# A recurrence over a graph: first gates' inputs copied earlier, one round fewer in the last sub-block, base sums spread 2,1,2,2,2,2,2,3, and another order of the filler tasks

## The chip, the core and the metric

The kernel runs on one core of a Trainium2 chip. The metric is the device time of one execution in microseconds, the median of several runs. A profile is one execution; its span is the time from the first to the last instruction.

## What is computed

Four layers work on node features `x` [16, 1024, 256] and a weighted adjacency `adj` [16, 1024, 1024]; each layer adds its result to `x`, after a layer norm and a ReLU. The change touches layer 2 only, a recurrence over the nodes in their order:

```python
norm_adjT = jnp.swapaxes(adj, 1, 2) * dinv[:, :, None]

def step(h, i):
    x = jnp.take(h_e, i, axis=1)
    row = jnp.take(norm_adjT, i, axis=1)
    x_par = jnp.einsum('bj,bjd->bd', row, h)
    iou = x @ W_ioux.T + b_ioux + x_par @ W_iouh.T + b_iouh
    r, z = jnp.split(iou, 2, axis=1)
    r, z = (jax.nn.sigmoid(r), jax.nn.sigmoid(z))
    hc = jnp.tanh(x @ W_coux.T + b_coux + x_par * r @ W_couh.T + b_couh)
    h_new = z * x_par + (1.0 - z) * hc
    h = jax.lax.dynamic_update_slice(h, h_new[:, None, :], (0, i, 0))
    return (h, None)
h_out, _ = jax.lax.scan(step, h_e, jnp.arange(n))
```

About 3% of the entries of `adj` are not zero, so most nodes that stand near each other don't depend on each other.

## The kernel before

Layers 0 and 1 run from the start to about 1510 us, the recurrence to about 3455 us, layer 3 to the end. Everything is float32.

**Blocks and sub-blocks.** The 1024 nodes are 8 blocks (`t`) of 128. Within a block the nodes of each batch element are put into an order, worked out on the chip from `adj` (`orders`), and cut into 8 sub-blocks (`s`) of 16 nodes; for 16 batch elements a sub-block has 256 columns. Nodes that depend on each other are kept in different sub-blocks where that is possible. Where it isn't, a sub-block holds chains of nodes, and a chain of n nodes needs n rounds: a round (`round_`, from line 831) computes gates and new states of all columns from the present guess of `x_par`.

**Rounds.** `KS` (line 27) says how many rounds of each sub-block stand in the program, `CUTS` (line 28) at which column the second and later rounds begin, since the first nodes of a chain are done by then. For the eighth sub-block these are five rounds: one of 16 columns per batch element, two from column 4 on, two from column 12 on. If a block's data need more, `one_more` (line 876) repeats a whole round of all 256 columns, under the `If` of lines 1014 to 1017. How many are needed is in `more`, computed by `orders` from the chains.

**Order of work.** The order on PE, DVE, ACT and POOL is the order in which the Python code issues instructions (`tc.manual_schedule`, line 898). In each round PE has matmuls for `pr` and `pz` (each 4, recorded as 8 in a profile), then ACT and DVE make the sigmoid and the product for `pc`'s right side, PE does `pc`, ACT the tanh, DVE `w` and `hT` (lines 860, 861), PE four transposes (`turned`, line 865), ACT copies to `h` or `dh`. While ACT and DVE do their part PE is given other work from a list of tasks, `todo`. `fill(weight)` (line 953) takes tasks from it in order: a share before the first round, a share behind `pc`, the rest behind the transposes. The kinds of tasks, by the names used below:

- *base* (line 637): one of the matmuls that sum the earlier and later blocks' states for the next block, a chain of seven for one batch element, and a *turn* (line 651), two transposes. `BASES` (line 29) says how many batch elements each sub-block has. Base reads `hb`, which is loaded by SP's DMA queue, in part from `hs_d`, where the last sub-block's states of the block before have just been scattered (line 1030, POOL).
- *gates* (line 749): `x @ W` for a later sub-block, three tasks, each read from `hs`, a copy that POOL makes (line 740) of one sub-block of `he`.
- *far* (line 784): what the sub-block just done gives to later columns of the same block; *last* (line 687): what the last sub-block of the block before gives.
- *next* (line 771): what a sub-block gives to the first sub-block of the next block, into `pnx`.

Each base chain, turn, gates, far and last task holds one of three PSUM tiles named `pf`, from its first matmul until DVE or ACT has evicted it. The evictions (line 787 on DVE for far, 652 for turn, 624 on ACT for base) are put into a list, `late`, and issued at `evict()`, which stands before the sigmoids, behind the last `hT`, and behind the copies to `h`.

The gates of sub-blocks 2 to 7 and of the next block's first are issued at the end of the sub-block before, in the two arms of the `If`. Those of sub-block 1 are made in the gaps of sub-block 0: `Gates(he, 1)` at line 936 issues POOL's two copies there, and the three tasks come behind the first six base tasks. POOL's queue also carries the scatters, the gathers of `aj` (line 714), masks of `ab` (line 615) and the products `bd`, `ai` (lines 730, 721).

Of the kernel before, what the change touches and what calls it, by code (L numbers as in the profile page):

```python
# [16 lines left out]
P = 128  # L17
# [4 lines left out]
S = 16  # L22
NS = P // S
G2 = 2
GB = B // G2
GR = GB * S
KS = (1, 1, 1, 1, 1, 2, 2, 5)
CUTS = {5: (8,), 6: (8,), 7: (4, 4, 12, 12)}
BASES = (1, 1, 2, 2, 2, 2, 2, 4)
LN_EPS = 1e-5  # L30
RMS_EPS = 1e-6
DEG_EPS = 1e-5
# [8 lines left out]
def gnn_stack(ctx: ExitStack, tc: tile.TileContext, a: dict, out: bass.AP):  # L41
# [65 lines left out]
    def orders(pool, psum):  # L107
# [9 lines left out]
        def tile_(name, n=P):  # L117
            return pool.tile([P, n], F32, name="o_" + name)
# [39 lines left out]
        def rest():  # L158
# [47 lines left out]
            found = tile_("held", S)[:, :1]  # L206
            for s, cuts in CUTS.items():
                for k, cut in enumerate(cuts):
# [21 lines left out]
            for s in range(NS):  # L230
                nc.vector.scalar_tensor_tensor(need[:, s], again[:, s], float(KS[s] - 1), need[:, s], op0=ALU.mult, op1=ALU.add)
            for k in range(2):
                left = pool.tile([1, NT, NS], F32, name="o_left")
                for s in range(NS):
                    nc.vector.tensor_scalar(left[:, :, s], need[:, s], float(KS[s] + k), 0.0, op0=ALU.subtract, op1=ALU.max)
                nc.vector.tensor_copy(more[k], left.rearrange("o t s -> o (t s)"))
# [325 lines left out]
    def layer_2(shared, early):  # L562
        with ExitStack() as st:
# [102 lines left out]
            def last_tasks(t, bxt):  # L666

                n = P - S
                loaded = {}

                def load(b0):
                    ao = big.tile([P, 4, n], F32, name="ao", bufs=3)
                    nc.sync.dma_start(ao, next_d[b0 : b0 + 4, t - 1].rearrange("b p i -> p b i"))
                    hr = big.tile([P, 4, D], F32, name="hr", bufs=3)
                    nc.sync.dma_start(hr, hs_d[t - 1][b0 // GB][b0 % GB * P : (b0 % GB + 4) * P]
                                      .rearrange("(b p) d -> p b d", p=P))
                    loaded[b0] = ao, hr

                def task(b):
                    def run():  # L680
                        b0 = b - b % 4
                        ao, hr = loaded[b0]
                        if b % 4 == 0 and b + 12 < B:
                            load(b + 12)
                        pl = psum.tile([P, DC, n], F32, name="pf", bufs=3)
                        for c in range(DC):
                            nc.tensor.matmul(pl[:, c], hr[:, b - b0, c * P : (c + 1) * P], ao[:, b - b0],
                                             start=True, stop=True)
                        to = bxt[:, :, b, S:]
                        return lambda: nc.vector.tensor_add(to, to, pl)  # L690
                    return 0.4, run
                for b0 in (0, 4, 8):
                    load(b0)
                return [task(b) for b in range(B)]

            def load_he(t):
                he = big.tile([P, DC, B, P], F32, name="he")
                for c in range(DC):
                    nc.sync.dma_start(he[:, c], heT_d[:, :, c, t * P : (t + 1) * P].rearrange("b p i -> p b i"))
                return he  # L700
# [66 lines left out]
            def next_block(h, bd, n, start):  # L767

                for c in range(DC):
                    for g in range(G2):  # L770
                        nc.tensor.matmul(pnx[:, c, g * GR : (g + 1) * GR], h[:, g, c * P : (c + 1) * P],
                                         bd[:, g, :, n : n + S], start=start and c == 0 and g == 0, stop=True,
                                         skip_group_check=True)

            def far_tasks(bxt, h, sub):


                bd, s = sub.bd, sub.s
                far = P - (s + 2) * S

                def task(g, c, b4):
                    def run():
                        pf = psum.tile([P, 4, far], F32, name="pf", bufs=3)
                        nc.tensor.matmul(pf, h[:, g, c * P : (c + 1) * P], bd[:, g, b4 : b4 + 4, S : S + far],  # L784
                                         start=True, stop=True)
                        to = bxt[:, c, g * GB + b4 : g * GB + b4 + 4, P - far :]
                        return lambda: nc.vector.tensor_add(to, to, pf)  # L787
                    return 0.0067 * far, run
                tasks = []
                if far > 0:  # L790
                    tasks = [task(g, c, b4) for g in range(G2) for c in range(DC) for b4 in (0, 4)]
                if sub.n > P - s * S:
                    tasks.append((0.9, lambda: next_block(h, bd, P - (s + 1) * S, s == 0)))
                return tasks


# [68 lines left out]
            def turned(hT, fill, to):  # L865

                ph = psum.tile([P, DC, G2, P], F32, name="pa")
                for e in range(DC):
                    for g in range(G2):
                        nc.tensor.transpose(ph[:, e, g], hT[:, e, g * GR : (g + 1) * GR], ident)  # L870
                fill()
                for e in range(DC):
                    nc.scalar.activation(to[:, :, e * P : (e + 1) * P], ph[:, e], AF.Copy)
                evict()
# [23 lines left out]
            with tc.manual_schedule(engines={mybir.EngineType.PE, mybir.EngineType.DVE, mybir.EngineType.Activation, mybir.EngineType.Pool}):  # L898
                he = load_he(0)
# [12 lines left out]
                gx.seed_r()  # L912
                gx.seed_zc()

                near = None
                behind = []
                for t in range(NT):
                    if t == NT - 1:
# [9 lines left out]
                    for s in range(NS):  # L928


                        ahead = (t, s + 1) if s + 1 < NS else (t + 1, 0)
                        K = KS[s]
                        share = [task for _ in range(BASES[s] if base_todo else 0) for task in base_todo.popleft()]
                        todo, gx_next = [], None
                        if s == 0:
                            gx_next = Gates(he, 1)
                            todo = share[:6] + [(1.72, task) for task in gx_next.tasks] + share[6:] + behind
                        else:
                            if s == 1 and t + 1 < NT:
                                he_next = load_he(t + 1)  # L940
                            if s == 1 and t > 0:
                                for g in range(G2):
                                    nc.sync.dma_start(hn_d[g * GB : (g + 1) * GB, (t - 1) * P : t * P],
                                                      hs_d[t - 1][g].rearrange("(b p) d -> b p d", p=P))
                            lists = [behind, share]
                            sizes = [len(x) for x in lists]
                            while any(lists):
                                i = max(range(2), key=lambda i: len(lists[i]) / max(sizes[i], 1))
                                todo.append(lists[i].pop(0))
                        total = sum(cost for cost, _ in todo)  # L950
                        spent = part = 0.0
# [23 lines left out]
                        def rest_if(last, weight):  # L975
                            return lambda: fill(1.0 if last else weight * unit)

                        hT = work.tile([P, DC, G2 * GR], F32, name="hT", bufs=1)
                        h = work.tile([P, G2, D], F32, name="h")
                        rx = round_(x, x, None, 0, None, rest_if(False, 1.3), hT)  # L980
                        gx_now, gx = gx, gx_next
                        if s > 0 and sub_next:
                            nc.gpsimd.tensor_copy(tick, rx[:, DC - 1, :1])
                            gx = Gates(he if ahead[0] == t else he_next, ahead[1])
                        dh = h if K == 1 else work.tile([P, G2, D], F32, name="dh", bufs=1)
                        turned(hT, rest_if(K == 1, 0.5), dh)
                        if sub_next:
# [4 lines left out]
                        xs = x  # L992
                        for k, cut in enumerate(CUTS.get(s, ())):
                            last = k == K - 2
# [37 lines left out]
                        near = None  # L1032
                        if s + 1 < NS:
                            near = psum.tile([P, DC, G2 * GR], F32, name="pa")
# [4 lines left out]
                            behind = far_tasks(bxt, h, sub)  # L1039
                        elif t + 1 < NT:  # L1040
                            next_block(h, sub.bd, 0, False)
                            near = pnx
                            behind = last_tasks(t + 1, bxt_next)
                            bxt, he = bxt_next, he_next
# [171 lines left out]
    with tc.tile_pool(name="shared", bufs=2) as shared:  # L1216
        x, hn, at = {}, {}, {}
        layer_2(shared, lambda: early_3(shared, x, hn, at))
        layer_3(shared, x, hn, at)
# [46 lines left out]
```

## Time and profile before

| | |
|---|---|
| time, median of 3 runs | 4910.57 us (4909.06 to 4911.21) |
| span of the profiled execution | 4909.6 us, of a run of 4911.68 us |
| mean granted clock of TensorE | 0.970 |
| base matmuls, line 637 | 451.9 us busy, 1568 records |
| gates matmuls, line 749 | 352.4 us busy, 1536 records |
| far matmuls, line 784 | 224.3 us busy, 768 records |
| base's evictions on ACT, line 624 | 140 of 476 ns |

A group's busy time is the union of its instructions' spans on the engine; "idle before" is the time that the engine stood still just before one of them, with the instruction or DMA that ended it. A float32 matmul leaves two records. Times within the span are counted from its start. The cut into 40 slices, each 122.7 us long, shows PE at 7 to 9 tenths and more through the recurrence:

```profile
PE   8998899999997989898989898998799999999999
```

### The profile page before, as it was taken

The numbers are of one execution on the slowest core, as the hardware profiler recorded it, in microseconds if no ns is written. First come the engines' busy times: TensorE is split into PE (matmuls) and PEld (weight loads), VectorE is DVE, ScalarE is ACT, GpSimd is POOL, SyncE is SP. The second block draws the span as 40 slices with busy tenths as digits, with TensorE's granted clock in tenths as the row PEclk, the third lists the DMA queues.
The fourth block names the chain that finished last, engine by engine and source line by source line (L and its number), as shares of the span: only waits on it lengthen the run. The fifth ranks groups of instructions, "written<-read, shape, count | busy, mean of one in ns | idle before, by whom it ended". The sixth has DMA issues, their size and how long they took to land. (4 is left out here: it accounts for less than half of the span.)

```text
span 4909.6 us, 52727 instructions
## 1 busy us (share of the span) xinstructions
PE 4521.0 (92%) x18307; PEld 3029.4 (62%) x18307; DVE 2288.1 (47%) x6408; ACT 1218.7 (25%) x2651; POOL 1584.7 (32%) x1947
## 2 busy tenths in 40 slices
PE   8998899999997989898989898998799999999999
PEld 4443445555555878787777777777465555555656
DVE  6667744465553444444444444444524334344342
ACT  1211112222111223222322222223322323223232
POOL 3222233443333322232222232332524334234231
PEclk9999999999998999999999999999899999999999
DMA  4333325545536444444343444431412222222200
GB/s 156 113 96 103 88 85 201 188 167 178 174 117 187 128 151 126 135 141 141 114 145 109 147 130 149 128 131 35 167 69 86 77 92 72 77 103 71 75 26 17
DMA packets 530980, 576.65 MB, mean 117 GB/s; under 512 B 42544, under 2 KB 439472, under 8 KB 528304
## 3 DMA queue, kind: packets, MB, share of 16 engines
q1 hardware_dynamic: 499536, 460.27, 30.2%
q0 software_dynamic: 31040, 111.44, 6.3%
q8 instruction: 199, 3.26, 0.3%
q14 instruction: 205, 1.68, 0.1%
HBM read 469.65 MB, written 116.65 MB: 119 GB/s over the span
## 5 line engine op out<-in xcount | busy, mean ns | idle before, releaser
L309 PE MATMUL pa<-at,h 128*128 128x512 f32 x1088 | 498.4, 611 | 32.8 <-DVE ag L314 32.8
L637 PE MATMUL pf<-hb,ab 128*128 128x256 f32 x1568 | 451.9, 401 | 72.2 <-DMA hb<-hs_d 44.6
L1141 PE MATMUL ph<-ag,w 128*128 128x512 f32 x1024 | 479.0, 611 | 32.6 <-DVE hh L1145 32.5
L1179 PE MATMUL po<-w,hh 128*128 128x256 f32 x2048 | 447.7, 379 | 0.0
L1179 PEld LDWEIGHTS po<-w,hh 128*128 128x128 f32 x2048 | 387.8, 190 | 59.3 <-issue 7.9
L309 PE MATMUL pa<-at,q 128*128 128x512 f32 x960 | 424.3, 595 | 0.0
L309 PEld LDWEIGHTS pa<-at,h 128*128 128x128 f32 x1088 | 210.5, 196 | 278.7 <-issue 232.9
L749 PE MATMUL pf<-hs,wx 128*128 128x256 f32 x1536 | 352.4, 384 | 16.0 <-POOL hs L740 16.0
L637 PEld LDWEIGHTS pf<-hb,ab 128*128 128x128 f32 x1568 | 289.1, 201 | 126.1 <-DMA hb<-hs_d 46.8
L1141 PEld LDWEIGHTS ph<-ag,w 128*128 128x128 f32 x1024 | 178.8, 190 | 293.8 <-DVE hh L1145 150.7
L1147 POOL TENSOR_TENSOR ss<-ss,sq 128x512 f32<-128x512 f32 x224 | 304.7, 1360 | 115.9 <-ACT sq L1144 111.6
L749 PEld LDWEIGHTS pf<-hs,wx 128*128 128x128 f32 x1536 | 294.4, 193 | 57.7 <-POOL hs L740 17.1
L309 PEld LDWEIGHTS pa<-at,q 128*128 128x128 f32 x960 | 178.2, 190 | 216.6 <-issue 212.8
L754 DVE TENSOR_TENSOR gates<-pf,bias 128x512 f32<-128x512 f32 x128 | 88.4, 690 | 373.7 <-PE pf L749 363.8
L1145 DVE TENSOR_SCALAR hh<-ph,b 128x512 f32<-128x512 f32 x256 | 189.8, 746 | 152.7 <-ACT sq L1144 118.1
L784 PE MATMUL pf<-bd,h 128*128 128x384 f32 (+5 forms) x768 | 224.3, 379 | 26.6 <-DVE bxt L787 26.6
L1126 PE MATMUL pa<-bxt,h 128*128 128x512 f32 x512 | 227.6, 597 | 18.5 <-POOL bxt L1108 18.5
L1030 POOL DMA_INDIRECT hs_d<-h,table x128 | 129.1, 1009 | 313.7 <-ACT gates L757 220.9
L1126 PE MATMUL pa<-at,h 128*128 128x512 f32 x512 | 227.0, 594 | 0.0
L1144 ACT ACTIVATE sq<-ph,b 128x512 f32<-128x512 f32 x224 | 153.9, 687 | 229.7 <-PE ph L1141 184.5
L1171 ACT ACTIVATE hh<-hh,rw 128x512 f32<-128x512 f32 x256 | 168.9, 714 | 138.2 <-DVE hh L1170 136.5
L1182 DVE TENSOR_TENSOR x<-x,po 128x256 f32<-128x256 f32 x120 | 50.4, 420 | 289.0 <-PE po L1179 289.0
(253 smaller groups left out, 7406.7 us busy)
## 6 DMA issues: line engine op xcount, KB each, us to landing
at<-in_adjT SPq DMA_DIRECT2D x64, 1024.0 KB
ab<-in_adj SPq DMA_DIRECT2D x128, 512.0 KB
bxt<-in_adjT SPq DMA_DIRECT2D x64, 512.0 KB
at<-in_adjT SPq DMA_DIRECT2D x64, 512.0 KB
ad<-in_adj SPq DMA_DIRECT2D x128, 128.0 KB
x_d<-x POOLq DMA_DIRECT2D x16, 1024.0 KB, 4.8
he_d<-h POOLq DMA_DIRECT2D x16, 1024.0 KB, 9.0
heT_d<-hT POOLq DMA_DIRECT2D x16, 1024.0 KB
```

The lines of the kernel that those rows point to most:

```text
L309: nc.tensor.matmul(pa, h[:, mt, c * P : (c + 1) * P], at[n0 // 512][:, mt], start=mt == 0, stop=mt == NT - 1)
L637: nc.tensor.matmul(pb, ab[:, jts[k]], hb[:, jts[k]], start=k == 0, stop=k == len(jts) - 1)
L749: nc.tensor.matmul(pg[:, e], wx[:, c, q * D + e * P : q * D + (e + 1) * P], self.hs[:, c], start=c == 0, stop=c == DC - 1)
L784: nc.tensor.matmul(pf, h[:, g, c * P : (c + 1) * P], bd[:, g, b4 : b4 + 4, S : S + far], start=True, stop=True)
L1030: nc.gpsimd.indirect_dma_start(out=hs_d[t][g][:, :], out_offset=row(1, g, t, s), in_=h[:, g], in_offset=None)
L1126: nc.tensor.matmul(pa, h[b][:, mt, c * P : (c + 1) * P], at[b][n0 // NH][:, mt], start=mt == 0, stop=mt == NT - 1)
L1141: nc.tensor.matmul(ph, w1[:, c, k * P : (k + 1) * P], ag[:, c, n0 : n0 + NH], start=c == 0, stop=c == DC - 1)
L1144: nc.scalar.activation(sq, ph, AF.Square, bias=b1[:, k : k + 1])
L1145: nc.vector.tensor_scalar(hh[:, k], ph, b1[:, k : k + 1], None, op0=ALU.add)
L1147: nc.gpsimd.tensor_tensor(ss, ss, sq, ALU.add)
L1171: nc.scalar.activation(hh[:, k], hh[:, k], AF.Silu, scale=rw[:, k : k + 1])
L1179: nc.tensor.matmul(po, hh[:, c, k * P : (k + 1) * P], w2[:, c], start=c == 0, stop=c == HC - 1)
```

## The change

The copy of `hs` for the gates of a block's sub-block 1 is issued one sub-block earlier: in the eighth sub-block of a block POOL copies `hs` for the first two sub-blocks of the next block, and the three gates tasks stand first in sub-block 0's list. (The first block has no block before it; its copy stays where it was.) The eighth sub-block has four rounds in the program, not five; the second round from column 12 on is left out. `one_more` is decided against the new number, so what is computed stays the same. One batch element's base chain moves from the eighth sub-block to the first. In the lists of the other sub-blocks *next* stands first and not last, and in sub-blocks 1 to 4 the seventh to tenth tasks are base tasks.

```diff
-KS = (1, 1, 1, 1, 1, 2, 2, 5)
-CUTS = {5: (8,), 6: (8,), 7: (4, 4, 12, 12)}
-BASES = (1, 1, 2, 2, 2, 2, 2, 4)
+KS = (1, 1, 1, 1, 1, 2, 2, 4)
+CUTS = {5: (8,), 6: (8,), 7: (4, 4, 12)}
+BASES = (2, 1, 2, 2, 2, 2, 2, 3)
...
                 if sub.n > P - s * S:
-                    tasks.append((0.9, lambda: next_block(h, bd, P - (s + 1) * S, s == 0)))
+                    tasks.insert(0, (0.9, lambda: next_block(h, bd, P - (s + 1) * S, s == 0)))
                 return tasks
...
-                near = None
+                near = gx_ahead = None
...
                         if s == 0:
-                            gx_next = Gates(he, 1)
-                            todo = share[:6] + [(1.72, task) for task in gx_next.tasks] + share[6:] + behind
+                            gx_next = gx_ahead or Gates(he, 1)
+                            todo = [(1.72, task) for task in gx_next.tasks] + share + behind
...
                                 i = max(range(2), key=lambda i: len(lists[i]) / max(sizes[i], 1))
+                                if K == 1 and share and 6 <= len(todo) < 10:
+
+                                    i = 1
                                 todo.append(lists[i].pop(0))
...
                             gx = Gates(he if ahead[0] == t else he_next, ahead[1])
+                            gx_ahead = Gates(he_next, 1) if s + 1 == NS else None
```

## The prediction

> **What bounds the kernel now.** I write (t,s) for sub-block s of block t, both from 0. First the page's busy times: PE is the engine to follow.
>
> ```profile
> PE 4521.0 (92%) x18307; PEld 3029.4 (62%) x18307; DVE 2288.1 (47%) x6408; ACT 1218.7 (25%) x2651; POOL 1584.7 (32%) x1947
> ```
>
> Then the list of PE's waits over the recurrence (waited for, us in total, times, longest): a load at each block's start, and evictions of `pf`.
>
> ```profile
> PE pf L637 <- DMA hb<-hs_d: 44.6, 6, 9.1
> PE pf L784 <- DVE bxt L787: 26.6, 39, 1.5
> PE pf L637 <- ACT bs L624: 18.9, 18, 1.2
> ```
>
> PE's timeline at the starts of blocks 1 and 5 (start, length, records, in brackets the idle time before): *next* ends, base stands at the queue's head and its load isn't there. In block 5 four base matmuls could go first.
>
> ```profile
> 1753.03 1.05 PE L771 MATMUL pnx<-bd,h 128*128 128x128 f32 x8
> 1761.99 4.33 PE L637 MATMUL pf<-hb,ab 128*128 128x256 f32 x12 [7.91 <-DMA hb<-hs_d]
> ...
> 2775.84 1.89 PE L637 MATMUL pf<-hb,ab 128*128 128x256 f32 x8
> 2785.08 2.08 PE L637 MATMUL pf<-hb,ab 128*128 128x256 f32 x4 [7.35 <-DMA hb<-hs_d]
> ```
>
> The fifth round of (1,7): PE's work, with filler in its gaps.
>
> ```profile
> 1740.48 1.08 PE L827 MATMUL pa<-ai,dh 128*128 128x32 f32 x8 [0.38 <-ACT dh L873]
> ...
> 1742.08 1.00 PE L802 MATMUL pr<-dx,wh 128*128 128x64 f32 x8
> ...
> 1745.03 1.95 PE L637 MATMUL pf<-hb,ab 128*128 128x256 f32 x8
> 1746.81 0.60 PE L870 MATMUL pa<-ident,hT 128*128 128x128 f32 x4
> ```
>
> (2,5) behind `pc`: filler keeps PE busy until the transposes; DVE's chain ends with `hT` and only then evicts.
>
> ```profile
> 2151.29 0.59 PE L637 MATMUL pf<-hb,ab 128*128 128x256 f32 x2
> 2151.72 0.39 PE L784 MATMUL pf<-bd,h 128*128 128x128 f32 x2
> ...
> 2153.47 0.67 PE L870 MATMUL pa<-ident,hT 128*128 128x128 f32 x4
> ...
> 2153.22 0.42 DVE L861 TENSOR_TENSOR hT<-z,w 128x256 f32<-128x256 f32 x1
> 2153.57 0.48 DVE L787 TENSOR_TENSOR bxt<-bxt,pf 128x128 f32<-128x128 f32 x2
> ```
>
> Last, two windows of 3.4 us in (1,3): length, busy PE, PEld, DVE, ACT, POOL, then granted clock. PE half idle in one, half the clock in the next.
>
> ```profile
> 1847.00:1850.40 3.40, 1.65 (x7) 0.82 (x6) 2.38 (x7) 1.39 (x4) 0.00 (x0) 0.99 0.60 167
> 1850.40:1853.80 3.40, 3.40 (x11) 2.67 (x10) 1.35 (x4) 0.00 (x0) 0.29 (x1) 0.51 0.80 257
> ```
>
> [...] of the full-clock windows of that length in the recurrence, all 24 with at least 1.6 us idle are followed by one at 0.50, and 3 of the 227 others. [...] the eviction at 2153.57 stands behind `hT`. [...] (1,3) waits 1.05 us for line 624 and 0.70 us for line 787, and nearly every (t,2) to (t,4) does the like.
>
> **Part by part**, against the profiled span of 4909.6 us; the runs' median, 4910.57, is 1.0 us above it.
>
> *Fifth round out.* In (1,7) its starts give 0.92 + 2.95 (1742.08 to 1745.03) + 0.44 for the transposes, 4.3 us of PE, and 0.1 us of its wait, since the remaining filler is thinner. Blocks 0 to 6: 7 × 4.4 = 31. Block 7 has no filler: transposes of round four at 3441.87, of round five at 3452.43, 10.6. Together −41.4.
>
> *Repeats.* Following `orders` on the input arrays gives the rounds each sub-block needs. With the old numbers that makes six repeats, (1,4), (3,2), (3,3), (3,4), (4,3), (4,4), just where the trace has them. The eighth sub-block needs 5, 4, 4, 5, 5, 3, 5, 5 rounds: with four in the program, blocks 0, 3, 4, 6, 7 repeat. A repeat in (1,4) takes 15.1 us from the transposes at 1881.91 to the next sub-block's matmul at 1896.98, of which 1.76 filler and 5.2 gates are there without it: +8.1. In the eighth there is less filler before it, one turn of 0.3 against the copies' 1.0: +0.7. Four × 8.8 = 35.2. Block 7 has no gates for the gaps and starts at half clock: 0.8 + 1.9 + 1.1 to its `pr`, 6 for eight matmuls `pr`, `pz` and four `pc` (5.2 at full clock, the first 2 us at half[...]), 2.3 and 0.9 to the end: 13.0 (11 at full clock, 17 at half). Together +48.2.
>
> *Gates first.* Three gates, 5.2 us (1747.82 to 1753.03 in (0,7)), now stand between *next* and base. I count from the start of *next*: PE reaches base at 0.9 + 5.2 = 6.1. The load came at 9.0, 10.6 and 10.0 in blocks 1 to 3; behind a repeat the scatter is 1.3 us later against PE (1896.25 before 1896.98 in (1,4); 1750.96 before 1753.03 in (0,7)). With 0, 1 and 2 base matmuls free of the load, the waits of 7.9, 9.1, 8.1 become 4.2, 4.1, 3.1. In blocks 4 to 6 the three base matmuls before `pr` don't need it, and the fourth stands behind 5.2 us of round, at 12.6, after the load: 6.1, 7.4, 6.0 go. Sum −33.2. Block 7 loses POOL's wait of 0.7; block 0 gains 1.8 and loses 1.5, because a turn now delays its tanh: −1.0. Should the loads come 2 us later, 6 of it is lost. The moved copies are 2 × 0.36 us of POOL, which idles 4.8 us there (to 1712.06).
>
> *Base moved.* A chain and its turn are 3.4 us of PE in both places: 0. SP now issues the third chain's loads (1.4 MB, 4.3 us at the 330 GB/s of 1760 to 1765) in sub-block 0, ahead of the fourth `ao`, `hr`; lasts wait for that pair for 7.0 us in all seven blocks. They stand later now: 0, at most +4. The third mask is one more wait in POOL's queue, ahead of products that need `dh`, 10 us later: 0.
>
> *Order.* I read the changed program's order with its semaphores. s=1: four base matmuls come first behind `pc`, so the third far arrives after its eviction: −0.55. s=2: where a chain's turn is filled in together with its last base matmul, line 624 is issued ahead of the tanh and holds it up (1821.18 before 1821.55 in (1,2), against 1819.84 without). That matmul now comes first behind `pc`, not behind a far and a base, 0.97 us earlier; the waits of 0.94 and 0.77 shrink to about 0.7 and 0.8: −0.3. s=3, 4: 0. s=7: only *next* before `pr`, which waits for `x`: +0.2. **s=5 and 6:** behind `pc` stand far, turn, base, far, and the second far needs the first's tile, whose eviction stands behind the second `hT`. Counted from 2151.29, PE is there at 0.23 + 0.27 + 0.43 = 0.93, the eviction ends at 2.56, its signal some 0.07 later: a wait of 1.7 where none was. In the second round a far waits for a turn's eviction in the same way: 1.36 against 2.12 (s=6: 1.29), 0.8. (2,5) had two waits of 0.32 and 0.48 that go. So s=5 +1.7, s=6 +2.4; seven blocks (the eighth has no base): 7 × (−0.55 − 0.3 + 0.2 + 4.1) = +24.2. From below 12, if half is hidden; from above 32.
>
> *Clock.* Blocks 4 to 6 lose their slow windows at the start, about 2 us each, blocks 1 to 3 little: −7. The 1.7 us waits are at the threshold of 1.6: half of 14 slow the next window, at 1.5 us ((t,4) without repeats takes 26.4 or 24.8, with and without): +10; s=2, now below it, −3. Sum 0; bounds ±20.
>
> Sum: −41.4 + 48.2 − 33.2 − 1.0 + 24.2 = −3.2; from the median, 4907.
>
> **Rivals.** *The new waits don't open* (order, faster): if evictions overtake or the filler shifts, −24 − 4 and −10 of clock, 4869; past a quarter of it the kernel is faster. For: everything else is sound as counted. Against: DVE's order.
> *Slow windows take over* (slower): all 14 new waits and all 21 in s=2 to 4 (14 now) halve the next window. That is 7 + 2 + 7 = 16 windows more than counted, 24 us, 4931; from nine on it is slower. For: the waits lie within 0.1 us of the threshold, and sub-blocks of 27.2 us are nearly eight windows, so phases repeat. Against: 7 of 21 escape now.
> *The fifth round was not needed*: 41 − 48 becomes −41, 4859. The inputs say it is.
>
> **Numbers.** No change, within 0.2% (9.8 us, what a measurement of this kernel can tell): 0.43, 4901 to 4920. New waits smaller or absent: 0.33, with the third rival 0.35. Slow windows: 0.22. So 4907; the range reaches 16 us below the band's end, where half of the faster case lies, and 10 above: 4885 to 4930.
>
> **What would show it.** Line 637's wait for `hb` near 11 us, in blocks 1 to 3 only; five more repeats, in (t,7); far (line 784) waiting 1.7 us for line 787 in (t,5), (t,6); (t,7) near 44 us in blocks 1, 2, 5 and 53 in 0, 3, 4, 6, from 52.2. Wrong if waits in s=5, 6 stay below 1 us, or block starts still wait 8.

## The result, and the profile after

The changed kernel takes 4859.33 us (median of 4 runs, 4853.81 to 4864.38) against 4910.38 us for the kernel before (4909.06 to 4911.21): a ratio of 0.9896, with a 95% interval of 0.9879 to 0.9913. That is 51 us less, where 4907 was predicted and the range ended at 4885. The profiled execution has a span of 4858.2 us, 51.4 less than before (4909.6), and a mean granted clock of 0.978 instead of 0.970.

The page's line of busy times shows 26 us less busy time on PE; the base, gates and far matmuls themselves are the same in number.

```profile
PE 4494.9 (93%) x18199; PEld 3004.6 (62%) x18199; DVE 2303.1 (47%) x6354; ACT 1220.2 (25%) x2629; POOL 1586.6 (33%) x1939
```

The list of PE's waits over the recurrence (waited for, us in total, times, longest). The wait for `hb`, which led the list with 44.6 us, is down to 7.4 us in the last line shown (a third such wait, of 2.5 us in block 1, is put down to issue); far's waits for line 787 are fewer and longer, 18 instead of 39, and 26.5 us in all as before (26.6); waits for `hr` have grown from 7.0 to 11.8 us.

```profile
PE pf L784 <- DVE bxt L787: 26.5, 18, 1.6
...
PE pf L687 <- DMA hr<-hs_d: 11.8, 7, 2.3
...
PE pf L637 <- DMA hb<-hs_d: 7.4, 2, 3.9
```

PE's timeline at the start of block 2 (start, length, operation, in brackets the idle time before). The gates come first, one base matmul runs, and the next stands waiting for the load, ahead of `pr`, for 3.9 us.

```profile
1989.75 4.91 PE L749 MATMUL pf<-hs,wx 128*128 128x256 f32 x22
1994.50 0.59 PE L637 MATMUL pf<-hb,ab 128*128 128x256 f32 x2
1998.99 2.07 PE L637 MATMUL pf<-hb,ab 128*128 128x256 f32 x4 [3.89 <-DMA hb<-hs_d]
2000.86 2.50 PE L802 MATMUL pr<-x,wh 128*128 128x256 f32 x8
```

PE's timeline in (1,3) behind `pc`, and then two windows of it (length, busy PE, PEld, DVE, ACT, POOL, granted clock, DMA). The two waits are 0.61 and 0.90 us where they were 1.05 and 0.70, and the window behind them stays at full clock, where it fell to 0.51 before.

```profile
1843.04 0.70 PE L784 MATMUL pf<-bd,h 128*128 128x256 f32 x2 [0.61 <-ACT bs L624]
1844.64 0.70 PE L637 MATMUL pf<-hb,ab 128*128 128x256 f32 x2 [0.90 <-DVE bxt L787]
```

```profile
1841.67:1845.08 3.41, 1.89 (x8) 1.03 (x7) 2.63 (x8) 1.32 (x4) 0.00 (x0) 1.00 0.62 184
1845.08:1848.49 3.41, 3.41 (x20) 2.91 (x19) 1.44 (x4) 0.17 (x1) 0.29 (x1) 1.00 0.75 231
```

PE's timeline in (2,5) behind `pc`, and DVE's beside it: the new wait is there, in the place that was predicted, and at the price: the second far wants the first one's tile, whose eviction at 2129.61 stands behind the second `hT`.

```profile
2127.34 0.38 PE L784 MATMUL pf<-bd,h 128*128 128x128 f32 x2
...
2129.95 0.49 PE L784 MATMUL pf<-bd,h 128*128 128x128 f32 x2 [1.57 <-DVE bxt L787]
```

```profile
2129.27 0.43 DVE L861 TENSOR_TENSOR hT<-z,w 128x256 f32<-128x256 f32 x1
2129.61 0.28 DVE L787 TENSOR_TENSOR bxt<-bxt,pf 128x128 f32<-128x128 f32 x1
```

PE's timeline of the eighth sub-block of block 1: the fourth round's `pc`, filler, and the transposes at 1735.67; no round follows.

```profile
1732.78 1.28 PE L802 MATMUL pc<-drx,wh 128*128 128x64 f32 x8
...
1735.67 0.60 PE L870 MATMUL pa<-ident,hT 128*128 128x128 f32 x4
```

The trace of before records the granted clock of PE in 100 stretches, that of after in 72. All but the last of each are, to 0.1 us, whole numbers of 3.413 us long, and each is granted either 1 or 0.5. I call 3.413 us of such a stretch a window. In windows granted 0.5 the matmuls start half as often: from one record of 256 columns to the next it is 427 ns in both traces, and 216 ns at full clock (medians over lines 637, 749 and 802). For the reading below I split PE's time over the recurrence (from the first matmul for `pr` to the last transposes) into three: idle time; the loss to half clock, which is half of the busy time in windows granted 0.5; and the rest, work. The recurrence is 54.0 us shorter, of which idle 25.1 (185.1 to 160.1), half clock 27.6 (54.9 to 27.3), work 1.3. In the same way each sub-block:

| | before | after |
|---|---|---|
| (t,0), blocks 0 to 6: idle, us | 63.9 | 28.7 |
| (t,0), blocks 0 to 6: loss to half clock | 14.2 | 5.0 |
| (t,1) to (t,4), blocks 0 to 6: idle | 53.1 | 46.0 |
| (t,2) to (t,4), blocks 0 to 6: loss to half clock | 23.9 | 3.4 |
| (t,5) and (t,6), blocks 0 to 6: idle | 11.9 | 35.2 |
| (t,5) and (t,6), blocks 0 to 6: loss to half clock | 0 | 0 |
| (t,7), all blocks: time | 417.5 | 390.3 |

So half of the gain between these two traces came from a term that the prediction had put at 0. The experiments take the change apart first, then the clock.

### The profile page after: what moved, and what is told of

It reads as the page before. It is cut to its first block, busy times and chain, and to the rows that moved or that the text cites. A ratio compares the mean times of both kernels' runs of the same rounds, so it can differ in the third digit from the quotient of the medians.

```text
span 4858.2 us, 52472 instructions
## 1 busy us (share of the span) xinstructions
PE 4494.9 (93%) x18199; PEld 3004.6 (62%) x18199; DVE 2303.1 (47%) x6354; ACT 1220.2 (25%) x2629; POOL 1586.6 (33%) x1939
## 5 line engine op out<-in xcount | busy, mean ns | idle before, releaser
L637 PE MATMUL pf<-hb,ab 128*128 128x256 f32 x1568 | 420.6, 387 | 29.0 <-DVE bxt L787 16.2
L637 PEld LDWEIGHTS pf<-hb,ab 128*128 128x128 f32 x1568 | 278.2, 192 | 69.5 <-DVE bxt L787 23.4
L784 PE MATMUL pf<-bd,h 128*128 128x384 f32 (+5 forms) x768 | 214.4, 373 | 51.7 <-DVE bxt L787 26.5
L787 DVE TENSOR_TENSOR bxt<-bxt,pf 128x384 f32<-128x384 f32 (+5 forms) x384 | 141.2, 384 | 149.1 <-PE pf L784 146.6
```

The lines of the kernel that those rows point to most:

```text
L637: nc.tensor.matmul(pb, ab[:, jts[k]], hb[:, jts[k]], start=k == 0, stop=k == len(jts) - 1)
```

## The experiments: the parts

Each run is compared with runs of the kernel before on the same chip, whose median was 4907.6 us (rounds, gates, order, and more work in the waits), 4908.4 (the combinations, and the single pause), 4912.2 (four pauses, narrow work ahead) and 4907.7 (narrow work behind). Where a run is set against the changed kernel, or against another run, the chips can differ, and with them the time of one and the same kernel by some 5 us, as these medians show.

**Rounds alone.** The kernel before with four rounds in the eighth sub-block and nothing else.

```diff
-KS = (1, 1, 1, 1, 1, 2, 2, 5)
-CUTS = {5: (8,), 6: (8,), 7: (4, 4, 12, 12)}
+KS = (1, 1, 1, 1, 1, 2, 2, 4)
+CUTS = {5: (8,), 6: (8,), 7: (4, 4, 12)}
```

> From the kernel before, only the fifth round of the eighth sub-block is left out of the program (KS, CUTS; base stays 1,1,2,2,2,2,2,4). By the prediction's terms: -41.4 for the round, +48.2 for five repeats, so +7 us on the kernel before. By the profile after (a repeat costs 8.0 us there, an eighth sub-block without one is 9.2 us shorter of which 3.4 are the base chain that moved): 7 x -5.8 + 4 x 8.0 + 5 = -4 us. If the removed round were what gives the gain: -35 or more.

Measured: 4886.91 us, ratio 0.9962 (0.9949 to 0.9974): 21 us less, where +7 (the prediction's terms) or −4 (the profile after) was expected. In the trace a block without a repeat is 7.2 us shorter in (t,7), not 4.4: work −5.2 and idle −2.0. A block with a repeat gets 0.4 to 0.9 longer, so the repeat costs 7.6 to 8.1 us, not 8.8; block 7 gets 3.3 us longer. Together (t,7) loses 15.4 us. The two profiled executions differ by 23.2; most of the rest is half clock in (t,1) to (t,4), 17.1 us where it was 26.1, though the edit touches nothing there. The waits show where the missed idle time was. The fifth round has waits of its own, for `dh` before its `pa` and for `change` before its transposes: in the kernel before they came to 15.2 us (31 times) and 8.2 us (18 times), here to

```profile
PE pa L827 <- ACT dh L873: 8.6, 18, 0.9
...
PE pa L870 <- DVE change L861: 4.2, 11, 1.4
```

**Gates alone.** The kernel before with the copy of `hs` a sub-block ahead and the gates first.

```diff
-                near = None
+                near = gx_ahead = None
...
-                            gx_next = Gates(he, 1)
-                            todo = share[:6] + [(1.72, task) for task in gx_next.tasks] + share[6:] + behind
+                            gx_next = gx_ahead or Gates(he, 1)
+                            todo = [(1.72, task) for task in gx_next.tasks] + share + behind
...
+                            gx_ahead = Gates(he_next, 1) if s + 1 == NS else None
```

> From the kernel before, only the copy of hs one sub-block ahead and the three gates tasks first in sub-block 0's list. Prediction's terms: -33 us of waits for hb in blocks 1 to 6, and -7 of half clock there: -40 us. If the loads land later once PE comes later, or last tasks then wait for hr: -20 or less. The windows at half clock in sub-blocks 2 to 4 should stay as many as before, about 14.

Measured: 4831.53 us, ratio 0.9858 (0.9842 to 0.9875): 76 us less than before, where 40 was expected. This part of the change alone is 28 us faster than the whole. PE's timeline at the start of block 1 has no wait at all between *next* and `pr`, and no base matmul:

```profile
1746.33 1.05 PE L771 MATMUL pnx<-bd,h 128*128 128x128 f32 x8
1747.50 5.42 PE L749 MATMUL pf<-hs,wx 128*128 128x256 f32 x24
1752.76 1.89 PE L802 MATMUL pr<-x,wh 128*128 128x256 f32 x8
```

Idle time in (t,0) of blocks 0 to 6 falls from 63.9 to 13.9 us, and the half-clock loss of the whole recurrence from 54.9 to 24.6. Of that loss 11.9 us went at the block starts. But 17.1 went in (t,2) to (t,4), where 4 slow windows are left of 14, and the expectation that they stay as many was missed: the waits there are as long as before (47.4 us of idle time in both traces). The section on the clock comes back to this.

**Order alone.** The kernel before with *next* at the head of its list and the rule for the seventh to tenth task.

```diff
-                    tasks.append((0.9, lambda: next_block(h, bd, P - (s + 1) * S, s == 0)))
+                    tasks.insert(0, (0.9, lambda: next_block(h, bd, P - (s + 1) * S, s == 0)))
...
+                                if K == 1 and share and 6 <= len(todo) < 10:
+                                    i = 1
```

> From the kernel before, only the order: next first in the lists, base at places seven to ten in sub-blocks 1 to 4. If waits alone count (idle of the profile after against before): 7 x (-0.6 -0.4 -0.3 -0.2 +1.4 +1.9) = +13 us. If the clock counts, and the half-clock windows of sub-blocks 2 to 4 go because their waits fall under 1.6 us: about 20 us less than that, -7 us, with no more than 3 such windows in sub-blocks 2 to 4.

Measured: 4904.74 us, ratio 0.9995 (0.9986 to 1.0003): no change that can be told. In the trace this is a sum of two that cancel: idle +13.1 us, half clock −15.4 ((t,2) to (t,4) alone −18.8, from 23.9 to 5.1). The new waits are as long as predicted: idle +1.4 to 1.5 us in each (t,5), +1.9 to 2.0 in each (t,6).

**Gates and rounds, without the other two parts.** Both diffs above.

> The kernel before with two of the four parts only: gates first with the copy of hs a sub-block ahead, and four rounds in the eighth sub-block. The spread of the base sums and the order of the other lists stay as they were. If the parts add up as they were measured alone (-76 and -21 us), 4811 us. If they share a gain (both take idle time and half-clock windows near the turn of a block), up to 20 us of it is had only once: 4811 to 4831. If the moved base and the new order were what the change needs to bring the gates' gain out, it should stand near the changed kernel, 4859. By the sums of the prediction (-34 and +7): 4880.

Measured: 4823.77 us, ratio 0.983 (0.9818 to 0.9843). The two parts add up to within 13 us, inside the 20 allowed for a shared gain, and give 36 us more than the whole change. The moved base sums and the new order together cost about that much.

**Without the base move.** The changed kernel with the base sums spread as before.

```diff
-BASES = (2, 1, 2, 2, 2, 2, 2, 3)
+BASES = (1, 1, 2, 2, 2, 2, 2, 4)
```

> The changed kernel with the base sums spread 1,1,2,2,2,2,2,4 as before; gates first, four rounds and the new order stay. Theory: with two chains in sub-block 0 the first share of the list reaches three base matmuls ahead of pr, one of which needs hb, so PE waits for the load again; with one chain nothing but gates stands there. Idle time before line 637 on hb falls by about 15 us, time 4844 us (4838 to 4850). The prediction's own term for the base move is 0: 4859 us. Rival: the fourth chain in the eighth sub-block costs as much there as it saves: 4855 to 4865.

Measured: 4825.32 us, ratio 0.9834 (0.9821 to 0.9846): the base move costs 34 us, over twice the 15 that I expected even after the result. PE's timeline at the start of block 2 now goes from the gates straight to `pr`:

```profile
1977.80 5.35 PE L749 MATMUL pf<-hs,wx 128*128 128x256 f32 x24
1982.98 1.89 PE L802 MATMUL pr<-x,wh 128*128 128x256 f32 x8
1984.71 1.89 PE L802 MATMUL pz<-x,wh 128*128 128x256 f32 x8
```

The traces of the two differ by 31.1 us in the recurrence: idle 18.9, work 6.8, half clock 5.4. The idle time has 9.9 in the three waits for `hb` (2.50, 3.89 and 3.53 in blocks 1, 2 and 3 of the changed kernel, none here), 4.7 in the waits for `hr` (11.8 there, 7.1 here), and 3.3 in one wait in (3,1) that is put down to issue; the trace of the changed kernel with one pause (below) doesn't have that wait, so it isn't a cost of the move. The work is the chain itself: with it (t,0) of blocks 0 to 6 has 3.0 to 3.8 us more work, while (t,7) has 2.4 less, and in most blocks is only 1.9 to 2.1 us shorter, because there the chain stood partly in time that PE had to wait anyway.

**The new order only where there is one round.** As the last run, but *next* last again in (t,5) and (t,6).

```diff
+                            if K == 2:
+                                behind = [*behind[1:], behind[0]] if t + 1 < NT else behind
```

> As the run with the base spread of before, and in the two sub-blocks with two rounds next stands last in its list again, as before; only the sub-blocks with one round, and the eighth, keep the new order. Theory: the waits of 1.5 us and 0.6 us for line 787 in those two sub-blocks go, seven blocks times 3.3 us = 23 us less than the run with the new order everywhere: about 4821 us. Against the run with gates and rounds alone it tells what the new order is worth in the sub-blocks with one round: 0 if its only gain (half-clock windows) is had already from the others, up to -10 us if it isn't. Rival: the waits only move to another place of the same sub-blocks: no difference to the run with the new order everywhere.

Measured: 4797.25 us, ratio 0.9773 (0.976 to 0.9785), the fastest of all. Against the last run that is 28 us, where 23 was expected: idle falls by 1.2 to 1.5 us in each (t,5) and 1.9 to 2.0 in each (t,6), as much as the order alone had put there. Far's waits for line 787 are down from 26.5 to 8.0 us, and line 652 isn't waited for any more:

```profile
PE pf L784 <- DVE bxt L787: 8.0, 11, 1.5
```

Against gates and rounds alone it is 27 us, more than the 10 that I allowed. The two traces differ by 20: 8.9 of idle time, most of it 0.2 to 0.6 us in every (t,1) to (t,4), 6.4 of half clock, 4.2 of work. So the order is worth something in the sub-blocks with one round even where the block starts are already mended.

## The experiments: the clock

**More work in the waits.** The kernel before; the second far matmul behind `pc` is issued twice in (t,2) and (t,3), three times in (t,4), into the same tile.

```diff
...
-                        nc.tensor.matmul(pf, h[:, g, c * P : (c + 1) * P], bd[:, g, b4 : b4 + 4, S : S + far],
-                                         start=True, stop=True)
+                        for _ in range(times):
+                            nc.tensor.matmul(pf, h[:, g, c * P : (c + 1) * P], bd[:, g, b4 : b4 + 4, S : S + far],
+                                             start=True, stop=True)
...
+                                if hasattr(task, "far") and fars == 2 and behind_pc and base_todo and 2 <= s <= 4:
+                                    late.append(task(3 if s == 4 else 2))
...
```

> From the kernel before; in sub-blocks 2 to 4 of blocks 0 to 6 the second far matmul behind pc is done twice (three times in sub-block 4), with the same result: PE gets 0.3 to 0.65 us more to do just ahead of the wait for line 624, 21 times. Clock theory: idle in a 3.4 us window falls from about 1.75 to 1.2 to 1.35 us, under the 1.6, so the 14 half-clock windows go and the kernel is 20 to 24 us faster although PE does more. Rival, that only waits and order count: the added work fills a wait, 0 us, or costs up to +11 us.

Measured: 4895.3 us, ratio 0.9977 (0.997 to 0.9984). PE has 13.1 us more work and 13.0 us less idle time, and the kernel is 12 us faster, about half of the 20 to 24 expected: the half-clock loss in (t,2) to (t,4) went from 23.9 to 0, but 4.1 more was lost at block starts. In (1,3) the first of the two waits, 1.05 us before, is cut to 0.61 by the repeated matmul, and the second, 0.70 before, is as long as before:

```profile
1846.46 0.70 PE L637 MATMUL pf<-hb,ab 128*128 128x256 f32 x2 [0.61 <-ACT bs L624]
1847.87 0.70 PE L785 MATMUL pf<-bd,h 128*128 128x256 f32 x2 [0.71 <-DVE bxt L788]
```

So the half-clock loss follows what PE does in the waits: work without any use removes it.

**A pause on DVE.** The changed kernel with a 128x128 copy, that nothing reads, between the last `hT` and the evictions of (t,2) to (t,6).

```diff
+                while hold:
+                    hold.pop()()
                 evict()
                 return r
...
+                        if 2 <= s <= 6 and t + 1 < NT:
+                            hold.append(lambda: nc.vector.tensor_copy(pause, ones))
```

> The changed kernel with one more 128x128 copy on DVE, into a tile that nothing reads, between the last hT and the evictions behind it, in sub-blocks 2 to 6 of blocks 0 to 6 (35 copies of about 0.2 us). It leaves PE's work as it is and lengthens the waits of 1.4 to 1.57 us for evictions to about 1.65 to 1.8 us, past the 1.6 us of idle time in a window behind which the clock was at half in the kernel before. Clock theory: up to 35 windows more at half clock at 1.0 to 1.6 us each beside the 35 times 0.2 us themselves: +30 to +60 us, 4890 to 4920, with the half-clock loss in sub-blocks 2 to 6 rising from 3 us to 25 or more. Rival, the wait costs its own length and no more: +7 to +9 us, 4867.

Measured: 4872.53 us (4867.06 to 4883.6), ratio 0.9933 (0.9922 to 0.9945), 13 more than the changed kernel, far from the 30 to 60 of the clock theory and somewhat over the rival's 7 to 9; its profiled execution has a span 6.9 us longer, with idle +3.5 and half clock +1.6. The waits grew by 0.1 us each only, but past 1.6 us, and the clock did not follow. Two windows of (2,5), in the columns used above: 1.71 us idle, and full clock after it.

```profile
2128.54:2131.95 3.41, 1.70 (x11) 1.25 (x10) 2.44 (x8) 0.66 (x2) 0.00 (x0) 1.00 0.00 0
2131.95:2135.37 3.42, 3.42 (x25) 2.96 (x23) 0.77 (x3) 1.13 (x3) 0.89 (x3) 1.00 0.00 0
```

So 1.6 us of idle time in a window doesn't part the slow from the full here: 10 windows of this trace had over 1.65 us and were followed by full clock. I formed another theory, to be tried on the runs: that the clock follows how many columns PE's matmuls work through. From rows as `pr` (8 records of 256 columns in 1.73 us, 1982.98 to 1984.71 above) a record takes its columns at about 1.2 per ns. So I call a record's columns, divided by 1.2 per ns, its streaming time, and spread it evenly over the span that the profile gives the record; a window's streaming time is the sum of what falls into it.

**The same pause four times.**

```diff
-                            hold.append(lambda: nc.vector.tensor_copy(pause, ones))
+                            hold += [lambda: nc.vector.tensor_copy(pause, ones)] * 4
```

> As the run with one pause copy on DVE behind the last hT, with four such copies in a row (the one lengthened PE's waits by 0.1 us, not by the 0.2 expected; four should lengthen them by 0.4). The windows with the waits had 1.9 to 2.0 us without a streamed column under one copy; with four they come to 2.2 to 2.3, past 2.15 wherever the waits lie in one window. Clock theory: own length 35 x 0.4 = 14 us, and 15 to 30 more windows at half clock in sub-blocks 2 to 6 at about 1.5 us each, 22 to 45 us: 36 to 59 us over the changed kernel, 4895 to 4918. Rival, waits cost their own length only: 4873.

Measured: 4932.44 us, ratio to the kernel before 1.0048 (1.0035 to 1.0062); 73 us more than the changed kernel, above what either theory gave. The dose was larger than meant: DVE's timeline has 1.00 us for the four,

```profile
2133.74 1.00 DVE L989 COPY pause<-ones 128x128 f32<-128x128 f32 x4
```

and each sub-block 0.9 us more idle time, 35 × 0.9 = 32 us. The rest is clock: the half-clock loss rises by 37.1 us, in (t,2) to (t,6) from 3.4 to 41.5. Over these 35 sub-blocks the longer wait cost about twice its length.

**Narrow work in the waits.** The kernel before, with two matmuls of 16 columns, first ahead of the second far matmul behind `pc`, and in another run behind it. They keep PE busy about as long as the repeated full ones, and stream almost nothing. (The lines of the first form; in the second they stand below the full matmul.)

```diff
+                        for _ in range(times):
+                            nc.tensor.matmul(pf[:, 0, :S], h[:, g, c * P : (c + 1) * P], bd[:, g, b4, S : 2 * S],
+                                             start=True, stop=True)
...
```

> The kernel before with two more matmuls of 16 columns ahead of the second far matmul behind pc, in sub-blocks 2, 3 and 4 of blocks 0 to 6 (42 matmuls, 84 records of some 0.13 us, by line 827's eight of 32 columns in 1.08). The full matmul behind them writes the same tile anew, so nothing changes in what is computed. They fill about as much of PE's waiting time as the repeated full matmuls did (0.5 us of each sub-block's two waits), but stream 2 x 2 x 16 columns where those streamed ten times as many. Theory A, the clock follows the time in which PE is busy: the half-clock loss in sub-blocks 2 to 4 goes from 24 us to under 5, as with the repeated full matmuls, and the time to about 4896. Theory B, it follows the columns streamed (in all runs so far a window of 3.41 us with over 2.15 us in which no column is streamed[...], is followed by one at half clock, 81 of 87 such windows and none of those below 2.1): the filled windows go from 2.31 to about 2.26 us only, 14 of 21 stay, the half-clock loss stays at 18 to 27 us, the time within 6 us of before.

Measured, ahead: 4896.94 us, ratio 0.997 (0.9958 to 0.9982), half-clock loss in (t,2) to (t,4) 3.4 us. These are theory A's numbers, and B's expectation missed. But B had been worked wrongly: the pair moved the full matmul behind it some 0.4 us further into the waiting window, which streamed more by that. Hence the second form.

> As the run with narrow matmuls, but each pair of 16 columns stands behind the full far matmul and not ahead of it (it computes the first 16 columns of that tile once more, to the same values). In the first form the pair pushed the full matmul itself 0.5 us later, so more of its columns fell into the window of the waits, and these came to 2.04 to 2.17 us without a streamed column, not to 2.26: the run could not tell the two theories apart. Here the full matmul stays where it was, and the pair lies in the wait behind it. Theory A, the clock follows PE's busy time: idle time of the windows goes from 1.75 to about 1.3 us, the half-clock loss in sub-blocks 2 to 4 from 24 us to under 5, the time to about 4897. Theory B, it follows the columns streamed: the windows go from 2.31 to about 2.25 us without a streamed column, over the 2.14 at which all runs together part best; at least 10 of 14 windows stay at half, the loss stays at 17 to 27 us, the time within 6 us of before.

Measured, behind: 4898.68 us, ratio 0.9985 (0.9978 to 0.9991); half-clock loss in (t,2) to (t,4) 13.7 us. The time lies between the two theories, and 8 windows stayed at half where B wanted at least 10. How many windows the waits slow depends on where these fall, as shown below; so the count decides little, and the windows themselves decide: 8 of them with 1.36 to 1.44 us of idle time were followed by half clock, though their idle time is under 1.6 us. In (1,3) PE was busy for 2.01 us, more than the 1.70 of the window shown for the single pause, and the next was at half:

```profile
1845.92:1849.33 3.41, 2.01 (x11) 1.43 (x10) 2.29 (x7) 1.39 (x4) 0.00 (x0) 1.00 0.51 154
1849.33:1852.75 3.42, 3.42 (x10) 2.68 (x9) 1.44 (x4) 0.00 (x0) 0.29 (x1) 0.50 0.76 255
```

What PE was busy with in it is in its timeline: four narrow records, and few full ones. It streams 1.17 us, the window with the pause 1.42.

```profile
1845.99 0.59 PE L784 MATMUL pf<-bd,h 128*128 128x256 f32 x2
1846.42 0.52 PE L787 MATMUL pf<-bd,h 128*128 128x16 f32 x4
1847.63 0.70 PE L637 MATMUL pf<-hb,ab 128*128 128x256 f32 x2 [0.69 <-ACT bs L624]
1849.03 0.96 PE L784 MATMUL pf<-bd,h 128*128 128x256 f32 x2 [0.71 <-DVE bxt L790]
```

**Where the windows fall.** Counted from the first instruction, the windows' borders lie elsewhere in each trace: 0.33 us past whole numbers of 3.413 us in the kernel before, 1.88 us in the changed kernel. So the same waits can fall into one window or be parted by a border. Four kernels have the old order in (t,2) to (t,4), and there the same idle time, 47.4 us in blocks 0 to 6: the kernel before, rounds alone, gates alone, and gates and rounds. They lose 23.9, 17.1, 6.8 and 10.2 us to half clock there. The four with the new order (changed kernel, order alone, without the base move, and the fastest one) lose 3.4, 5.1, 3.4 and 3.4. To part what the order does from where the borders fall I moved a window of 3.413 us along the traces in steps of 10 ns and took its smallest streaming time in each sub-block that no slow window touched; the averages are

| smallest streaming time, us | s=2 | s=3 | s=4 |
|---|---|---|---|
| old order (kernel before) | 1.13 | 1.09 | 1.05 |
| new order (changed kernel) | 1.56 | 1.32 | 1.08 |

The other three kernels with the old order agree with the kernel before to 0.01. In all traces together each window that streamed for less than 1.25 us was followed by half clock (last section). Against that figure the new order has taken s=2 and s=3 out of reach wherever the borders fall, s=3 narrowly. It has not taken out s=4, where, by an estimate from the moved window, about a third of all border positions would still give a slow one. All nine slow windows that the four traces with the new order have in (t,2) to (t,4) lie in (t,4).

## Why the prediction was wrong

Its sum was −3 us; the change gives −51. By its own terms, in us over the recurrence, from the traces (the rows overlap a little, and come from different kernels, so they sum only roughly):

| term | predicted | measured |
|---|---|---|
| fifth round out, and repeats | +6.8 | −15.4, (t,7) with the rounds alone |
| gates first | −34.2 | −35.2, idle time of (t,0) in the changed kernel, blocks 0 to 6 |
| base moved | 0 | +31, of which 10 are the waits for `hb` that the term above allowed for, 5 clock, and 3 the wait in (3,1) |
| order, idle time in (t,1) to (t,6) | +22.8 (+24.2 with (t,7)) | +16.2 |
| clock | 0 | −27.6 |

*The clock* is the step that failed most. Its 0 was the sum of −7 at block starts, +10 for the new waits and −3 in s=2. At block starts −9.2 was measured, so that part was right. The prediction held that half of the 14 new waits of 1.7 us would slow the next window: none of the 14 did. And it held that s=3 and s=4 would keep their slow windows: of the 14 in s=2 to 4 (3, 6 and 5) two were left, both in s=4, which is −20.5 us. The 1.6 us of idle time, from which it worked, don't part the windows of these traces. In the trace of before, 24 of the 25 windows with that much idle time were followed by half clock and 3 of the other 502 (the prediction counted 227); but there the long waits all stood among much the same work, and idle time went along with streaming time. The new waits of (t,5) and (t,6) stand beside denser work: the eight windows there with over 1.5 us of idle time stream 1.40 to 1.64 us, the 14 of s=2 to 4 in the trace of before that half clock followed stream 1.06 to 1.21. The waits of s=3 got 0.2 to 0.3 us shorter, which the prediction's part *Order* had set at 0 because it is nothing in time, and that was enough: in (1,3) the window streamed 1.36 us after and 1.11 before.

Not all of the 20.5 is the change's doing. The 9 windows of s=2 and 3, 15 us, have no place left with the new order, in s=3 by a narrow margin. The three that went in s=4 are luck: its smallest streaming time is under 1.25 us before and after (1.05 and 1.08). And the kernel before stood badly: if the borders could fall anywhere, the shares of bad positions (0.25, 0.28 and 0.29 for s=2, 3 and 4) would give 5.7 slow windows in seven blocks, an estimate from its trace, and not 14. Whether other executions of it have as many isn't known, for only one was profiled. The rival *Slow windows take over* put a price on the wrong direction of the same mechanism; that a kernel whose windows stream so near 1.25 us (1.06 to 1.21) can as well come out on the good side is what the prediction lacked.

*Fifth round out* was mis-sized: 4.3 us of PE and "0.1 us of its wait" were in truth 5.2 and 2.0. I had taken its waits for filled once the filler was redistributed, while they belong to the round's own steps and go with it. *Repeats* had the right number, places and mechanism; 7.6 to 8.1 us instead of 8.8. Block 7, put at +2.4 (−10.6 and +13.0, in which 2 us at half clock were an estimate), got 3.3 longer with the rounds alone. That the fifth round is needed in some blocks, against the rival's 4859, is seen in the repeats; that the time met 4859 is chance.

*Gates first* was right in mechanism and size: the waits in blocks 1 to 3 were put at 4.2, 4.1 and 3.1 us and came to 2.5, 3.9 and 3.5, and those of blocks 4 to 6 went. But it was right for the change as a whole, second chain included. What the prediction didn't ask is what the gates would give without that chain: then nothing stands ahead of `pr` that needs the load, and 10 us more are to be had.

*Base moved*, at 0, failed in two places. "A chain and its turn are 3.4 us of PE in both places": 3.0 to 3.8 us of work in (t,0), but a gain of some 2 us in most of (t,7), where it lay partly in waits. And the waits for `hr`, "at most +4", grew by 4.7.

*Order* was right in s=5 and 6 (+1.7 and +2.4 predicted, +1.4 to 1.5 and +1.9 to 2.0 measured with the order alone), and a little too careful in s=3 and 4. The rival *The new waits don't open* is refuted: they did open, as the timeline of (2,5) shows. Whether more than three `pf` tiles would close these waits was not tried in any run.

## What to carry to other kernels

Before a wait is priced at its length, look at the clock of the window behind it: here a few tenths of a microsecond in s=2 and 3 were worth 15 us of clock, and useless work put into waits made the kernel 12 us faster. With windows that stream near 1.25 us the same waits cost 7 us in one kernel and 24 in another, so a clock loss read from a single trace is partly luck. Take a change of several parts apart: one part of this one gave more than the whole, and the best kernel keeps two parts, leaves out one, and applies the fourth only outside the sub-blocks with two rounds. Work moved to "where PE has it free" is not free twice: it costs its full length where there was no wait, and saves less where there was.

## What the runs showed of the hardware

Over all thirteen traces, the recurrence (from 1510 us to its last transposes) has 6878 windows of 3.413 us at full clock, 205 of them followed by one at half. By PE's idle time they part badly: of 206 windows with at least 1.6 us idle 163 are followed by half clock, and so are 42 of those with less, down to 0.97 us. By streaming time they part almost without exception: all 199 windows that stream for less than 1.25 us are followed by half clock; of the 6679 others 6 are, and these stream 1.26 to 1.32 us. In the traces of before and after alone it is all 39 of those below 1.25 us and 1 of the 1023 others, where idle time of at least 1.6 us gives 34 of 37 and 6 of 1025. These are counts over one kernel and its variants.

Other counts do worse, each taken with the limit that suits it best. Streaming time misjudges 6 windows, PE's busy time 67, the number of matmul records 101, the busy time of the weight loads 105; streaming time without the transposes misjudges 91, so transposes count here. Records of few columns keep PE busy in the profile, but hardly count: the four of 16 columns at 1846.42 above have 0.52 us on the timeline and 0.05 us of streaming time, and the clock behind their window was 0.50. The exact form of the count stays open, since the spans of matmuls, over which the columns are spread, are modelled in the profile.
